# Raw input normalising in a convolution: ScalarE's copy and GpSimd's low part two rounds behind the subtract

## The chip, the core and the metric

The kernel runs on one core of a Trainium2 chip. TensorE (PE; PEld is its weight load) multiplies matrices into PSUM. VectorE (DVE), ScalarE (ACT) and GpSimd (POOL) do the elementwise work, and SyncE (SP) issues the DMA transfers. Each engine takes the instructions of its own queue in order, and an instruction that waits for another engine's signal holds up what is queued behind it. The metric is the device time of one execution in microseconds (us): the median over runs.

## The reference

The input x has 8 batches of 2048 positions with 512 channels. Two blocks follow each other, each with a residual:

```
x = x + layernorm(s4(layernorm(x)))      # a long convolution per channel, then gelu
x = x + layernorm(ffn(layernorm(x)))     # a gated recurrence over the 8 batches, then tanh
```

`s4` builds one filter of 2048 taps for each of the 512 channels from a state of 64 complex numbers, convolves every channel with its filter and applies gelu. The first layernorm runs over the 512 channels, so each position and batch has a mean and a factor 1/sqrt(var + eps); the convolution's input is (x - mean) * factor. The feed-forward part isn't touched by the change.

## The kernel before

Positions are cut into NJ = 16 chunks of 128. Channels are cut into NG = 16 groups of G = 32, and a group is two slices of HS = 16 channels. A convolution of one channel is the product with a 128 x 128 matrix of taps inside a chunk (tile `t`), plus what earlier chunks left in the state (tile `x`, 256 columns: 32 channels by 8 batches), which is spread over the chunk by a second matrix (tile `m`). The state goes from chunk to chunk: this is "the chain". Values are kept as two float16 halves, a high half, which ScalarE copies (L101), and a low half, which VectorE subtracts (L102); a product of two such values takes three matmuls (`mm3`, L450 to L452).

The main loop (L801) runs over the groups g. While group g is convolved, the kernel prepares the next ones: the chain and the taps of group g + 1, and the input of group g + 2. A group has 16 steps s_ (L838). In order, a step emits

- every second step, the gelu of the four channels before (`conv_out`, L717, ACT)
- one or more pieces of the input's normalising (`norm_x`, L844, the part that the change touches)
- the convolution of two channels (`conv_mm`), with the chain's products in between: `chain_hi` (L661) after the first, `chain_lo` after the second. `chain_lo` of step j is one more product (L667), which needs the low half of the state of step j - 1, and then the split of its result: ACT's copy (L101) and VectorE's subtract (L102)
- in steps 1 to 12 a doubling of the next group's taps (`tap_step`: three products, L101, L102)
- the first products of the next chain step (`chain_in`)
- pieces of work on the feed-forward weights, on ACT and VectorE: L404 and L405 in step 2, L408 and L409 in step 5, L392/L393 in steps 8 and 12, L446 in step 14

The input of a group comes in two transfers of 1 MB (`load_x`, L629), each into one of two `xg` buffers with 8 chunks. A buffer is free for the next group when the last low part that reads it is done. Normalising goes in 8 rounds of two chunks, four of them in each buffer. A round r has four parts: GpSimd subtracts the mean (part 0, L641), VectorE multiplies with the factor (part 1, L643), ScalarE copies the high half into `u` (part 2, L645), GpSimd subtracts to get the low half (part 3, L647; for group 2 VectorE does it). They depend on each other in this order.

The list `norms` (L837) holds the parts in the order in which they are emitted, and L844 takes from its head as the steps go on, two in each step. With the lags of the kernel before, sub r comes in step 2r, mul r in 2r + 1, copy r in 2r + 2 and low r in 2r + 3; in the last step, 15, come mul 7, low 6, copy 7 and low 7. In group 1 the list starts at step 3 (`ND1`, L843), as its first input comes late. Groups 14 and 15 have no input to prepare. GpSimd's queue has one more kind of work, two copies of taps for each group (`load_taps`, L683), which overwrite tiles that the products of the group before have read.

The queues of PE, ACT, VectorE and GpSimd follow the written order within a group; between the end of one group and the start of the next, and on SP, a scheduler sets it. So on GpSimd the second L683 and sub 0 and sub 1 of the next group stand ahead of low 7 of the old one.

Of the kernel before, what the change touches and what calls it, by code (L numbers as in the profile page):

```python
# [24 lines left out]
NJ = L // P  # L25
# [34 lines left out]
def s4_gated_block(ctx, tc, a, dbg=None):  # L60
# [445 lines left out]
    def early_tiles():  # L506

        ya = early["y"] = [cb.tile([P, 2, H // HS, 2, HS], F32, name="ya", tag="m", bufs=4) for _ in range(2)]
        xa = cb.tile([P, 2, 2, H], F32, name="xra", tag="t0", bufs=3)
        xb = FJ.tile([P, 2, H], F32, name="xr", tag="wl"), FE.tile([P, 2, H], F32, name="xrb", tag="y")  # L510
        for cj in range(QC):
            early[cj] = ya[cj % 2][:, cj // 2], xb[cj // 2] if cj % 2 else xa[:, cj // 2]
        for cj in (0, 2, 1, 3):
            dma(out=early[cj][1], in_=a["r"][0:2, cj * P : (cj + 1) * P].rearrange("t p h -> p t h"))
            dma(out=early[cj][0][:, 0:SE], in_=y_d[cj, :, 0:SE, 0:2])

    def early_y(sl, y):

        v = y.rearrange("p (c b) h -> p c b h", b=NB)
        for i in range(2):  # L520
            Q.tensor_copy(early["y"][i][:, :, sl], v[:, i:QC:2, 0:2])
# [56 lines left out]
    JP = 2  # L578
    MAN = {mybir.EngineType.PE, mybir.EngineType.Activation, mybir.EngineType.DVE, mybir.EngineType.Pool}
    with ExitStack() as cctx:  # L580
# [44 lines left out]
        def load_x(g):  # L625
            us[g] = (cb, cr, ce)[g % 3].tile([P, NJ, 2, G, NB], F16, name="u", tag=f"u{g % 3}", bufs=1)
            for jq in range(NJ // JQ):
                xg = cr.tile([P, JQ, G, NB], F32, name="xg")
                dma(out=xg, in_=a["xr"][jq * JQ : (jq + 1) * JQ, :, g].rearrange("j p h b -> p j h b"))  # L629
                xgs[g, jq] = xg  # L630
# [18 lines left out]
        def chain_in(g, j):  # L649

            if j == 0:
                xs_[g] = (ce, cb)[g % 2].tile([P, NJ - 1, 2, GB], F16, name="x", bufs=1)
            u = us[g].rearrange("p j i h b -> p j i (h b)")
            pxs[g, j] = px.tile([P, GB], F32, name="pxt")
            mm3(pxs[g, j], lambda i: bm16[:, i, :], lambda i: u[:, j, i, :], stop=(j == 0))
# [18 lines left out]
        def load_taps(g):  # L674

            for sl in (2 * g, 2 * g + 1):
                t0 = cb.tile([P, 2, P, HS], F16, name="t0", bufs=3)
                base = kpad[:, sl, 1 : P + 1, :]
                tap = bass.AP(base.tensor, base.offset, [[HS, P], [2 * P * H, 2], [1, P * HS]])
                dma(out=t0.rearrange("p i t h -> p i (t h)"), in_=tap)  # L680
                t0s[sl] = t0
                m = cb.tile([P, 2, HS, P], F16, name="m", bufs=4)
                Q.tensor_copy(m[:, :, :, 0:4].rearrange("p i h k -> p i k h"), mb[:, :, :, sl * HS : (sl + 1) * HS])  # L683
                ms[sl] = m
# [10 lines left out]
        def tap_steps(g):  # L695
            steps = [(lv, k) for lv in range(2, LEV) for k in range(0, 1 << lv, min(1 << lv, 512 // HS))]
            return [(sl, lv, k) for lv, k in steps for sl in (2 * g, 2 * g + 1)]
# [23 lines left out]
        def weights(w):  # L721

            i = WORDER.index(w)
            wts[w] = (FW if i < 2 else FV if i == 2 else FT).tile([P, 2, 7, 2, BP], F16, name=f"w{w}", bufs=1)
            d = dma(out=wts[w], in_=wf_d[i])

        def conv_last(g):

            u, x = us[g], xs_[g]
            yt = {}  # L730
            for j0, j1, hn in ((0, JF, HS), (JF, NJ, 4)):
                n = j1 - j0
                for sl in (2 * g, 2 * g + 1):
                    t0, m = t0s[sl], ms[sl]
                    if j0 == 0:
                        yt[sl] = cb.tile([P, NJ * NB, HS], F32, name="y")
                    y = yt[sl][:, j0 * NB : j1 * NB]
                    for h0 in range(0, HS, hn):
                        pyt = py.tile([P, hn, n * NB], F32, name="pyt")
                        for hm in range(h0, h0 + hn):  # L740
                            hg = sl % 2 * HS + hm
                            o, c = pyt[:, hm - h0], NB if j0 == 0 else 0
                            mm3(o, lambda i: t0[:, i, :, hm], lambda i: u[:, j0:j1, i, hg, :], stop=False)
                            mm3(o[:, c:], lambda i: m[:, i, hm, :],
                                lambda i: x[:, max(j0 - 1, 0) : j1 - 1, i, hg * NB : (hg + 1) * NB], start=False)
                        S.activation(y[:, :, h0 : h0 + hn], pyt.rearrange("p h c -> p c h"), AF.Gelu, scale=unsc)  # L746
                    if j0 == 0:
                        early_y(sl, yt[sl])
                    dma(out=y_d[j0:j1, :, sl].rearrange("j p b h -> p j (b h)"), in_=y.rearrange("p (j b) h -> p j (b h)", b=NB))
                if j0 == 0:  # L750
                    early_row(0, (1,))

            for i in range(2):
                pt = [pm_.tile([P, KT, P], F32, name="pmt") for _ in range(2)]
                forms(0, 0, i, [normed[i], normed[i + 2]], pt)()
            early_row(1)
            for cj in range(QC):
                dma(out=x1_d[cj, :, 0], in_=early[cj][1][:, 0])
# [42 lines left out]
        for g in range(NG):  # L801
            nxt, nn = g + 1 < NG, g < NG - 2
            ahead = g > 0 and nxt
            if g == 1:
                FJ = ctx.enter_context(tc.tile_pool(name="fj", bufs=1, side="right", reuse_waits="tile"))
                c0r = FJ.tile([P, H], F32, name="c0r")
                dma(out=c0r, in_=a["c0r"])
                puc = FJ.tile([P, 3, KT], F32, name="puc")
            if g == NG - 2:
                rctx.close()  # L810
                FW = ctx.enter_context(tc.tile_pool(name="fw", bufs=1, side="right", reuse_waits="tile"))
                for w in range(2):
                    weights(w)
            if not nxt:
                ectx.close()
                FV = ctx.enter_context(tc.tile_pool(name="fv", bufs=1, side="right", reuse_waits="tile"))
                FE = ctx.enter_context(tc.tile_pool(name="fe", bufs=1, side="right", reuse_waits="tile"))
                fcol = FE.tile([P, 4, KT], F32, name="fcol")
            with tc.manual_schedule(engines=MAN if nxt else MAN | {mybir.EngineType.SP}):
                if ahead:  # L820
                    load_taps(g + 1)
                    if g == NG - 2:
                        mctx.close()
                    taps = tap_steps(g + 1)
                    chain_in(g + 1, 0)
                if nn:
                    load_x(g + 2)
                if not nxt:
                    early_tiles()
                    for sl in (2 * g - 2, 2 * g - 1):  # L830
                        early_y(sl, ys[sl])
                    dma(out=fcol, in_=a["fcol"])
                    weights(2)
                    early_row(0, (0,))
                    conv_last(g)
                    continue
                norms = [(k - lag, part) for k in range(NJ // JP + 1) for part, lag in ((0, 0), (2, 1), (1, 0), (3, 1))]  # L837
                for s_ in range(NJ):  # L838
                    if s_ % 2 == 0 and s_:
                        conv_out(g, s_ // 2 - 1)  # L840
                    if nn:

                        d = ND1 if g == 1 else 0  # L843
                        while norms and s_ >= d and (s_ == NJ - 1 or len(norms) > 4 + 2 * NJ * (NJ - 1 - s_) // (NJ - d)):  # L844
                            norm_x(g + 2, *norms.pop(0))

                    conv_mm(g, 2 * s_)
                    if ahead and s_ < NJ - 1:
                        chain_hi(g + 1, s_)
                    conv_mm(g, 2 * s_ + 1)  # L850
                    if ahead and s_ < NJ - 1:
                        chain_lo(g + 1, s_)
                    if ahead and 1 <= s_ <= 12:
                        tap_step(*taps[s_ - 1])
                    if ahead and s_ < NJ - 2:
                        chain_in(g + 1, s_ + 1)
                    for f in work.get((g, s_), ()):
                        f()
                conv_out(g, NJ // 2 - 1)
# [495 lines left out]
```

## Time and profile before

| | us |
|---|---|
| median of 3 runs | 2872.67 |
| lowest and highest run | 2871.69, 2873.89 |
| span of the profiled execution | 2869.6 |
| busy in the span: PE / PEld / DVE / ACT / POOL | 2567.3 / 2236.0 / 2097.3 / 1478.7 / 1213.1 |
| stretch 0 to 143 (statistics of the input, first chains) | PE busy 72.7 |
| stretch 143 to 577 (convolution with normalising) | PE 364.2, DVE 348.1, ACT 286.6, POOL 309.7 |
| stretch 577 to 640 (last groups of the convolution) | PE 49.2 |
| stretch 640 to the end (feed-forward) | PE 2081.2, DVE 1612.2 |

In the stretch of the change the four parts take, as means of one instruction: L641 1455 ns (96 of them from 200 to 580 us), L643 926 ns, L645 630 ns, L647 1235 ns. The shortest L643 of the whole run took 676 ns, the longest 1783.

A line of a timeline reads: start and duration in us, engine, line, operation, tiles out and in, partitions x elements and types, how many instructions are merged in it, and in brackets how long the engine stood idle before it and what ended that. A line of the waits reads: engine, tile and line that waited, the instruction it waited for, us in total, how often, and the longest.

### The profile page before, as it was taken

To read this page: it belongs to the slowest core of one execution; us is meant where nothing else is said; L and a number is where in the kernel's file an instruction comes from. 1 tells how busy PE (TensorE), PEld (TensorE's weight loads), DVE (VectorE), ACT (ScalarE), POOL (GpSimd) and SP (SyncE) were. 2 spreads that over 40 slices of the span, in tenths; PEclk is the share of its full clock that TensorE was granted. 3 is DMA by queue.
4 is the path that set the end of the run, shared out by engine and by line. 5 is a ranking of instruction groups with operands and counts; after the bars stand their busy time and mean duration, and the time that the engine had idled before them with its cause. 6 is when DMAs were issued, how large, how long until landed. Compare 5 with 4: busy or idle time off the path is not lost.

```text
span 2869.6 us, 60008 instructions
## 1 busy us (share of the span) xinstructions
PE 2567.3 (89%) x23940; PEld 2236.0 (78%) x23940; DVE 2097.3 (73%) x4248; ACT 1478.7 (52%) x3091; POOL 1213.1 (42%) x1496
## 2 busy tenths in 40 slices
PE   4588888876999999999999998999999999999991
PEld 3377777765888888778888886888888788888880
DVE  7878788837667766677777777777777677776758
ACT  8966666634344444445455544455454445544435
POOL 5776777613112221114554531355444124443317
PEclk8799999987999999999999999999999999999995
DMA  6978887797324333224565532355564235543356
GB/s 232 312 233 261 254 263 247 243 263 204 112 65 115 103 93 92 78 89 138 152 174 151 141 100 89 106 161 165 147 163 140 85 89 152 151 130 100 89 163 244
DMA packets 521937, 451.10 MB, mean 157 GB/s; under 512 B 289974, under 2 KB 401080, under 8 KB 516664
## 3 DMA queue, kind: packets, MB, share of 16 engines
q1 hardware_dynamic: 521224, 446.74, 52.4%
q8 instruction: 187, 3.06, 0.4%
q14 instruction: 94, 0.77, 0.1%
q10 hardware_dynamic: 432, 0.52, 0.1%
HBM read 295.41 MB, written 151.78 MB: 156 GB/s over the span
## 4 chain that ended last, share of the span: by engine, by line
PE 34%; DVE 9%; ACT 3%; DMA 2%; issue 1%; POOL 1%; SPq 0%; POOLq 0%; ACTq 0%; DVEq 0%
PE u L950 32%; PE pt L485 1%; DVE u L992 1%; DVE gate L1036 1%; DVE cf L1051 1%; DMA z_d<-zc 1%; ACT xf L101 1%; DVE cd L1037 1%; ACT gate L1016 1%; DVE sth L462 1%; DVE zz L1174 1%; DVE sty L462 1%; ACT y L903 0%; DVE u2p L989 0%; DVE xf L102 0%
## 5 line engine op out<-in xcount | busy, mean ns | idle before, releaser
L950 PEld LDWEIGHTS <-w 128*128 128x128 f16 x15120 | 1482.5, 98 | 217.2 <-issue 28.3
L950 PE MATMUL u<-xf,w 128*128 128x256 f16 x8064 | 947.6, 274 | 30.7 <-ACT zt L1003 12.7
L950 PE MATMUL u<-cf,w 128*128 128x256 f16 x7056 | 826.2, 273 | 3.8 <-DVE cf L1051 3.8
L988 ACT ACTIVATE u2p<-u 128x256 f32<-128x256 f32 x256 | 96.4, 378 | 449.8 <-PE u L950 449.6
L950 PE MATMUL u<-w,xf 128*128 128x256 f16 x2688 | 314.4, 275 | 14.8 <-DVE u L992 4.8
L989 DVE TENSOR_TENSOR u2p<-u2p,u 128x256 f32<-128x256 f32 x256 | 106.8, 417 | 285.8 <-ACT u2p L988 284.3
L1141 POOL TENSOR_TENSOR x1r<-x1r,zr 128x512 f32<-128x512 f32 x96 | 132.7, 1382 | 426.8 <-ACT zr L1140 309.4
L1016 ACT ACTIVATE gate<-u,bias 128x512 f32<-128x512 f32 (+1 forms) x384 | 200.5, 574 | 217.0 <-PE u L950 217.0
L950 PEld LDWEIGHTS <-xf 128*128 128x128 f16 x2688 | 264.6, 99 | 49.5 <-issue 10.7
L904 POOL TENSOR_TENSOR xr<-y,xr 128x512 f32<-128x512 f32 x120 | 160.4, 1357 | 308.2 <-ACT y L903 308.2
L992 DVE TENSOR_TENSOR u<-u,u2p 128x512 f32<-128x512 f32 x256 | 179.0, 699 | 8.8
L647 POOL TENSOR_TENSOR u<-xg,u 128x512 f16<-128x512 f32 x104 | 128.8, 1242 | 114.0 <-ACT u L645 113.9
L471 POOL TENSOR_TENSOR rsy<-rsy,nhalf 128x2 f32<-128x2 f32 (+1 forms) x68 | 50.9, 748 | 296.7 <-DVE rsy L465 284.4
L641 POOL TENSOR_TENSOR xg<-xg,mu 128x512 f32<-128x512 f32 x112 | 162.7, 1459 | 6.0 <-DMA xg<-in_xr 6.0
L102 DVE TENSOR_TENSOR x<-pxt,x 128x256 f16<-128x256 f32 x240 | 100.0, 418 | 63.2 <-ACT x L101 62.3
L1123 POOL TENSOR_TENSOR zr<-zr,ur 128x512 f32<-128x512 f32 x96 | 129.7, 1351 | 22.4 <-DMA zr<-z_d 16.6
L1021 DVE SCALAR_TENSOR_TENSOR gate<-gate,gate 128x1024 f32<-128x1024 f32 x64 | 93.4, 1459 | 59.8 <-ACT gate L1016 59.0
L462 DVE BATCH_NORM_STATS2 sty<-y 128x6 f32<-128x512 f32 x120 | 76.7, 681 | 72.7 <-DMA y<-y_d 72.7
L101 ACT ACTIVATE x<-pxt 128x256 f16<-128x256 f32 x240 | 91.5, 382 | 74.1 <-PE pxt L667 68.4
L101 ACT ACTIVATE xf<-pt 128x512 f16<-128x512 f32 x124 | 60.7, 489 | 133.4 <-DVE xf L102 114.4
L667 PE MATMUL pxt<-x,at 128*128 128x256 f16 x224 | 61.8, 276 | 75.1 <-DVE x L102 73.9
L450 PE MATMUL pyt<-u,t 128*128 128x128 f16 (+2 forms) x544 | 121.4, 223 | 5.4 <-ACT y L746 5.4
(371 smaller groups left out, 5319.1 us busy)
## 6 DMA issues: line engine op xcount, KB each, us to landing
xs<-in_rr SPq DMA_DIRECT2D x32, 1024.0 KB, 5.7
t<-kpad SPq DMA_DIRECT2D x32, 1024.0 KB, 5.6
y_d<-y SPq DMA_DIRECT2D x30, 1024.0 KB, 7.6
xr<-in_r SPq DMA_DIRECT2D x60, 512.0 KB, 5.5
xa<-x_d SPq DMA_DIRECT2D x120, 256.0 KB, 4.1
y<-y_d SPq DMA_DIRECT2D x59, 512.0 KB, 5.7
x_d<-xr SPq DMA_DIRECT2D x59, 512.0 KB, 3.2
xg<-in_xr SPq DMA_DIRECT2D x28, 1024.0 KB, 8.7
```

What stands on the lines that cost most here:

```text
L101: S.activation(hi, src, AF.Copy)
L450: T.matmul(out, lhsT=w(0), rhs=x(0), start=start, stop=False)
L462: V.bn_stats(st[:, i], v)
L641: Q.tensor_tensor(xg, xg, bc(mu1), ALU.subtract)
L647: (V if g == 2 else Q).tensor_tensor(u[:, js, 1], xg, u[:, js, 0], ALU.subtract)
L904: Q.tensor_tensor(xv, yv, xv, ALU.add)
L950: T.matmul(u[:, d], lhsT=w(f, b, i == 1, k), rhs=x(f, b, i == 2, k), start=opens and bank not in seen, stop=stop and j == len(n) - 1, skip ...
L989: V.tensor_tensor(u2, u2, u[:, UY], ALU.add)
L992: V.tensor_tensor(u[:, 2:4], u[:, 2:4], u2[:, None].to_broadcast([P, 2, BP]), ALU.add)
L1016: act = lambda o, s_, b: S.activation(o, s_, AF.Tanh, scale=gsc[kind], bias=b)
L1123: Q.tensor_tensor(s_["z"], s_["z"], us_[c], ALU.add)
L1141: Q.tensor_tensor(s_["x"], s_["x"], s_["z"], ALU.add)
```

## The change

The list of parts gets one more round, its order within a round changes, parts that don't exist are left out of the list, and the threshold of L844 loses its 4, as the list has 32 entries now for 36 before:

```
-norms = [(k - lag, part) for k in range(NJ // JP + 1) for part, lag in ((0, 0), (2, 1), (1, 0), (3, 1))]
+norms = [(k - lag, part) for k in range(NJ // JP + 2) for part, lag in ((2, 2), (0, 0), (1, 0), (3, 2)) if 0 <= k - lag < NJ // JP]
...
-    while norms and s_ >= d and (s_ == NJ - 1 or len(norms) > 4 + 2 * NJ * (NJ - 1 - s_) // (NJ - d)):
+    while norms and s_ >= d and (s_ == NJ - 1 or len(norms) > 2 * NJ * (NJ - 1 - s_) // (NJ - d)):
```

Worked out for a group from 2 to 13, step by step (s sub, m mul, c copy, l low):

```
step    0     1     2     3     4     5     6     7     8     9     10    11    12    13    14    15
before  s0    m0    s1c0  m1l0  s2c1  m2l1  s3c2  m3l2  s4c3  m4l3  s5c4  m5l4  s6c5  m6l5  s7c6  m7l6 c7l7
after   s0m0  s1m1  c0s2  m2l0  c1s3  m3l1  c2s4  m4l2  c3s5  m5l3  c4s6  m6l4  c5s7  m7l5  c6l6  c7l7
```

In the queues that result, PE's is the same. On GpSimd sub 0, sub 1 and sub 2 of the next group stand ahead of low 7 of the old one, and sub 4 stands ahead of low 2. On ACT copy 7 and the last gelu of a group stand ahead of the next group's first chain copy, which was ahead of them before. On SP the store of `y` (L719) and the load of L445 change places.

## The prediction

> **What bounds the kernel now.** I read the page for the span, then busy time by stretch, then who waited for whom within the convolution, and last the timelines of TensorE, VectorE, GpSimd and the load queue through one channel group. X(k) stands for the start of the chain's last product (L667) of step k, "mul r", "sub r", "copy r" and "low r" for L643, L641, L645 and L647 of round r, xlo(k) for the L102 subtract that X(k+1) needs.
>
> ```profile
> span 2869.6 us, 60008 instructions
> ```
>
> ```profile
> 293.50:325.05 31.55, 26.65 (x319) 22.96 (x318) 25.48 (x45) 21.01 (x46) 22.67 (x20) 1.00 0.82 255
> ```
>
> The second line is one channel group: length, then busy us (and instructions) of PE, PEld, DVE, ACT, POOL, then granted clock, DMA share, GB/s. Five such stretches in a row measure 31.50 to 31.55 us; the groups repeat like a clock, at a granted clock of 1.00, so one group can be worked out and multiplied. PE stands idle for 4.9 us of it. From 143 to 577 us, where the changed code runs, the waits are:
>
> ```profile
> ACT u L645 <- DVE xg L643: 69.5, 64, 1.8
> PE pxt L667 <- DVE x L102: 64.4, 61, 4.0
> ...
> DVE xg L643 <- POOL xg L641: 13.0, 13, 3.0
> ```
>
> ACT's copy waits 69.5 us for the multiply, PE waits 64.4 us for xlo, and the two look like one thing. The timelines say that they are not:
>
> ```profile
> 295.20 0.27 PE L667 MATMUL pxt<-x,at 128*128 128x256 f16 x1 [0.16 <-DVE x L102]
> ...
> 298.12 0.27 PE L667 MATMUL pxt<-x,at 128*128 128x256 f16 x1 [1.02 <-DVE x L102]
> ...
> 302.57 0.27 PE L667 MATMUL pxt<-x,at 128*128 128x256 f16 x1 [1.36 <-DVE x L102]
> ```
>
> ```profile
> 293.12 1.00 DVE L446 SCALAR_TENSOR_TENSOR un<-un,c0r 128x512 f32<-128x512 f32 x1
> 294.05 0.08 DVE L446 DVE_READ_ACCUMULATOR un<-un,c0r 128x1 f32 x1
> 294.05 0.77 DVE L643 TENSOR_TENSOR xg<-xg,rs 128x512 f32<-128x512 f32 x1
> 294.74 0.41 DVE L102 TENSOR_TENSOR x<-pxt,x 128x256 f16<-128x256 f32 x1
> 295.98 1.75 DVE L643 TENSOR_TENSOR xg<-xg,rs 128x512 f32<-128x512 f32 x1 [0.84 <-POOL xg L641]
> 297.65 0.41 DVE L102 TENSOR_TENSOR x<-pxt,x 128x256 f16<-128x256 f32 x1
> ```
>
> ```profile
> 292.41 1.16 POOL L647 TENSOR_TENSOR u<-xg,u 128x512 f16<-128x512 f32 x1 [2.42 <-ACT u L645]
> 293.51 1.24 POOL L683 COPY m<-mb 128x128 f16<-128x128 f16 x1
> 294.34 2.85 POOL L641 TENSOR_TENSOR xg<-xg,mu 128x512 f32<-128x512 f32 x2
> 297.14 2.74 POOL L647 TENSOR_TENSOR u<-xg,u 128x512 f16<-128x512 f32 x2
> 299.84 1.46 POOL L641 TENSOR_TENSOR xg<-xg,mu 128x512 f32<-128x512 f32 x1
> ```
>
> What ends last ahead of X(1), X(2) and X(4) is VectorE's queue: a multiply stands right before xlo. In this boundary between two groups the multiply at 294.05 is mul 7 of the old group and the one at 295.98 is mul 0 of the new one, which waits 0.84 us for sub 0 and then takes 1.75 us where others take 0.68, until sub 1 is over at 297.19. Other pairs read alike: L405 starts at 300.08 inside a GpSimd subtract (299.84 to 301.30) and takes 1.50 us, its sister L409 0.42. L102, which reads PSUM, stays at 0.41. So an operation of VectorE on two SBUF operands is held up while GpSimd works; that is the price list for the change.
>
> **The change part by part.** Eight multiplies, subtracts, copies and lows per group stay, and PE's queue is the same. Copy r and low r keep their steps (2r+2 and 2r+3, the last at 15). Sub and mul go one round ahead: mul r sat at step 2r+1 and now sits at 2r-1, with mul 0 at step 0 and mul 1 at step 1. On VectorE the places of the multiplies stay the same; each place has the next round's. Groups 2 to 13, twelve of them, are alike. All times below are on the clock of the timelines above.
>
> 1. *ACT's wait goes.* It is worth nothing. The copy that waited 1.23 us ran 302.22 to 302.85; the next in ACT's queue, the chain's own copy, started at 302.88, which is 0.31 after X(4)=302.57, the same lag as after 298.12 (298.42). It waited for PE, and PE for VectorE. Price if the cover were gone: up to the 64.4 us that PE waits.
>
> 2. *Sub 7 leaves step 13.* L393 (289.37 to 291.05, then mul, then xlo) overlapped it from 289.37 to 289.98. With GpSimd free there X(14), which waited 1.23 us, comes 0.6 earlier: 291.45 for 292.05. Between 0 and 0.6; I take 0.6.
>
> 3. *Mul 0 now stands before xlo(0), where mul 7 stood without a wait.* It waits for sub 0, which stands behind L683, which overwrites taps that the old group's last products read; those end with ACT's release at 293.02, now about 292.45. L683's spacing to the subtract is 0.83 (293.51 to 294.34): sub 0 from 293.3. One subtract takes 1.27 to 1.64 (294.34 to 295.98): mul 0 from 294.6 to 294.9. Sub 1 and sub 2 follow at once on GpSimd, so the nearest row is the 1.75 above: done by 296.5. From the start of xlo to X is 0.46 (294.74 to 295.20), so X(1) is 296.8 to 297.0 for 295.20, +1.7. Least: 0.68 for mul 0, +0.6. Queued behind mul 0 is xlo(0), and PE for it.
>
> 4. *Mul 1 stands before xlo(1)*, with sub 2 running: 0.68 to 1.75, so X(2) is 298.3 to 298.9 for 298.12 (before, the 0.84 wait and mul 0's 1.75 lay here). I take +0.6.
>
> 5. *Step 3: L404, L405, mul 2, xlo(3).* Before, GpSimd fell idle at 301.30 until low 1 at 302.92, which waited for the copy, which waited for mul 1; so mul 1 ran free in 0.68. Now copy 1 has its input long since and GpSimd has low 0, sub 3 and low 1 in a row, so each of the three VectorE operations may meet one. Nothing in the trace shows that place so filled. By the free rows +0, by the 1.75 row against 0.68 for the multiply +1.1 and by shifted overlaps of L404 and L405 +0.6 more. I take +1.3, nearer the filled row, since GpSimd is never idle there now. X(4): 304.5, +1.9.
>
> 6. *The second half's load.* Sub 4 needs the second xg buffer, freed by low 7. L629 issued it at 298.77, just when low 7 ended, and issues of that line in the groups beside it landed 7.3, 7.6, 8.7 and 8.9 us later; sub 4 started at 307.52, 8.75 after, so even now there is hardly room.
>
> ```profile
> 298.77 1.92 SPq L629 DMA_DIRECT2D xg<-in_xr  x1
> ```
>
> Now sub 4 is due a round sooner, right after low 1, while low 7 stands behind sub 2 and ends some 0.7 later (299.5). It lands at 306.8 to 308.4, sub 4 ends 1.27 later, mul 4 needs 0.68 to 1.75 before xlo(7), and X(8) is at least 309.2 to 311.9, for 309.37: -0.2 to +2.5. This delays the same xlo as part 5, so it is not added: the greater counts, and I take 2.0 for both. Behind the waiting sub 4 stand low 2, sub 5 and L683; on SP nothing new waits, only y's store and L445 change places.
>
> 7. *Step 9*, L393 and mul once more behind a shifted GpSimd: 0 to +0.6; I take 0. The first changed group (group 1, whose load is late anyway, a 3.99 us wait of PE) has mul 1 a step sooner: 0 to +1.3, I take 0.5. Group 0 has no chain: 0.
>
> Sum: 12 x 2.0 + 0.5 = 24.5 us on a span of 2869.6, so 2894.1. The median of the runs, 2872.67, lies 3.1 over the span; the same 3.1 gives 2897. After 577 us nothing changes, and nothing there makes up for a late start: it is one long run of PE (93% busy from 640 us on).
>
> [...]
>
> **The rivals.** *A, faster: the new waits are hidden.* Mul 0 gets its turn before sub 1 (+0.6 at X(1)), xlo(1) is then earlier than before, and only part 2 is left: 12 x -0.6 = -7, so 2866. For it: the 1.02 and 1.36 us of PE's waits at X(2) and X(4) are there to be eaten. Against: in the row shown sub 1 waits for nothing and was ahead, and mul 0 took 1.75 us. It decides if mul 0's mean at the boundary falls under 1 us and sub 4 does not wait. *B, no change:* the gain of part 2 pays for a stall of about 0.6 a group; 2868 to 2878. Against it: X(1) alone has 1.7. *C, the load rules:* each round of the load ends in a stall at X(8) at the long landing (2.5) and step 9 adds 0.6: 12 x 3.1 + 1.3 = 38.5, so 2911. For it: 8.75 us of the 8.9 are used up now. That the change doesn't do what it says I leave out: the built order of the engines has the multiplies one round ahead.
>
> **How the numbers follow.** Forecast 0.68, A 0.13, B 0.07, C 0.12. The likeliest gives 2897. Bounds of the forecast: 12 x 0.8 = 10 over (parts 3 to 5 at their least with a landing of 8.1) to 12 x 2.9 + 1 = 36 over: 2883 to 2909. Widened towards B and C: 2874 to 2912, which leaves out A, half of B and the end of C. This kernel's runs tell about 0.2% (5.7 us) from no change: faster 0.13, same 0.07, slower 0.80.
>
> **What would show it.** ACT's wait for L643 falls from 69.5 us to under 10, with no gain on PE; DVE's wait for L641 grows from 13 us to 25 or more; POOL's wait for the load grows from 6.0 us to over 20; the wait before X(1) grows from 0.16 to about 1.8 and that before X(14) falls from 1.23 to 0.6; the group's period is 33.5. I am wrong if the period stays under 31.6: then mul 0 found its subtract done, or the chain had slack that I don't see.

## The result, and the profile after

The changed kernel takes 2885.54 us (median of 5 runs, 2880.99 to 2886.13) against 2872.67 (5 runs, 2868.53 to 2874.30): 1.0043 times, with an interval of 1.003 to 1.0055. It is slower, by 12.9 us, where the prediction said 24. The profiled execution spans 2883.8 us, 14.2 more than the one before.

The waits of the changed kernel from 140 to 600 us (who waited for whom, us in total, times, longest):

```profile
ACT x L101 <- PE pxt L667: 143.9, 121, 3.5
...
PE pxt L667 <- DVE x L102: 69.5, 57, 4.1
...
POOL xg L641 <- DMA xg<-in_xr: 38.8, 13, 7.3
DVE xg L643 <- POOL xg L641: 21.4, 20, 3.0
...
ACT u L645 <- DVE xg L643: 4.6, 3, 3.9
```

ACT's wait for the multiply is gone (69.5 before, 4.6 now), and nothing was won by it: ACT now waits in the chain's own copy (143.9), and PE's wait for xlo is larger than before (64.7 in the same window). GpSimd waits for the second half's load in each group. TensorE through the changed kernel's X(8) of one group and X(14), X(1) and X(4) of the next:

```profile
284.83 0.27 PE L667 MATMUL pxt<-x,at 128*128 128x256 f16 x1 [1.26 <-DVE x L102]
...
298.84 0.27 PE L667 MATMUL pxt<-x,at 128*128 128x256 f16 x1 [0.75 <-DVE x L102]
...
304.02 0.27 PE L667 MATMUL pxt<-x,at 128*128 128x256 f16 x1 [2.18 <-DVE x L102]
...
310.16 0.27 PE L667 MATMUL pxt<-x,at 128*128 128x256 f16 x1 [1.36 <-DVE x L102]
```

X(14) of the kernel before:

```profile
292.05 0.27 PE L667 MATMUL pxt<-x,at 128*128 128x256 f16 x1 [1.23 <-DVE x L102]
```

Against the rows of before, the wait at X(14) fell from 1.23 to 0.75, the one at X(1) rose from 0.16 to 2.18, the one at X(2) (1.02) is gone, the one at X(4) (1.36) is as it was here, and X(7) or X(8) has a new one in eight of the twelve groups. VectorE, the same two groups:

```profile
282.81 1.63 DVE L643 TENSOR_TENSOR xg<-xg,rs 128x512 f32<-128x512 f32 x1 [1.53 <-POOL xg L641]
...
301.90 1.74 DVE L643 TENSOR_TENSOR xg<-xg,rs 128x512 f32<-128x512 f32 x1 [1.18 <-POOL xg L641]
...
303.89 1.43 DVE L643 TENSOR_TENSOR xg<-xg,rs 128x512 f32<-128x512 f32 x1
...
307.67 1.50 DVE L405 TENSOR_TENSOR ws<-wl 128x256 f32<-128x256 f32 x1
309.09 0.68 DVE L643 TENSOR_TENSOR xg<-xg,rs 128x512 f32<-128x512 f32 x1
```

and GpSimd:

```profile
281.50 1.28 POOL L641 TENSOR_TENSOR xg<-xg,mu 128x512 f32<-128x512 f32 x1 [4.27 <-DMA xg<-in_xr]
...
300.26 4.51 POOL L641 TENSOR_TENSOR xg<-xg,mu 128x512 f32<-128x512 f32 x3
304.73 2.73 POOL L647 TENSOR_TENSOR u<-xg,u 128x512 f16<-128x512 f32 x2
307.42 1.46 POOL L641 TENSOR_TENSOR xg<-xg,mu 128x512 f32<-128x512 f32 x1
309.16 1.62 POOL L647 TENSOR_TENSOR u<-xg,u 128x512 f16<-128x512 f32 x1 [0.28 <-ACT u L645]
```

The row at 301.90 is mul 0: it waits 1.18 us for sub 0 and is then held for 1.74 us beside subs 1 and 2, and xlo(0) and PE wait behind it. The row at 303.89 is mul 1, held beside sub 2 and low 7. The row at 309.09, mul 2, runs free in 0.68 us: sub 3 ended at 308.88, and GpSimd waited for copy 1 until 309.16. The row at 281.50 is sub 4, 4.27 us late because of the load; mul 4 (282.81) waits for it, and X(8) (284.83) for mul 4.

So that kernels can be compared by place, the table cuts a group at the starts of L667. Each number is a mean over the twelve groups 2 to 13, read from the timeline of TensorE. "Half clock" counts the groups in which PE ran at half its clock (granted 0.50) for 3.4 us, of which more below. The medians stand against 2868.4 to 2868.8 us for the kernel before in the same runs on the chip; only the first two rows are from the runs of the result.

| kernel | median us | ratio, 95% interval | X(14) to X(1) | to X(2) | to X(4) | to X(10) | to X(14) | group | half clock |
|---|---|---|---|---|---|---|---|---|---|
| before | 2872.67 | 1 | 3.18 | 2.92 | 4.45 | 11.81 | 9.19 | 31.55 | 0 |
| after | 2885.54 | 1.0043, 1.003 to 1.0055 | 5.17 | 1.91 | 4.26 | 12.50 | 8.72 | 32.55 | 5 |
| sub 7 only | 2862.05 | 0.9977, 0.9968 to 0.9986 | 3.12 | 2.87 | 4.45 | 11.85 | 8.72 | 31.02 | 0 |
| mul 0 first | 2887.92 | 1.0061, 1.0049 to 1.0074 | 5.97 | 1.96 | 4.00 | 11.81 | 9.19 | 32.93 | 8 |
| short load | 2875.14 | 1.0016, 1.0007 to 1.0025 | 5.17 | 1.98 | 4.19 | 11.95 | 8.72 | 32.00 | 8 |
| subs ahead | 2891.2 | 1.0078, 1.0065 to 1.009 | 3.13 | 2.87 | 5.51 | 13.12 | 8.72 | 33.34 | 9 |
| muls 0, 1 later | 2887.92 | 1.0068, 1.0056 to 1.0081 | 2.83 | 2.36 | 5.96 | 13.17 | 8.72 | 33.04 | 8 |
| late slots | 2855.9 | 0.9956, 0.9943 to 0.9969 | 3.64 | 1.72 | 4.46 | 12.24 | 8.39 | 30.45 | 0 |
| subs first | 2873.25 | 1.0017, 1.0008 to 1.0026 | 3.64 | 1.72 | 5.55 | 12.36 | 8.39 | 31.66 | 6 |
| L393 free | 2849.83 | 0.9932, 0.9919 to 0.9946 | 3.64 | 1.73 | 4.46 | 10.87 | 9.26 | 29.96 | 0 |
| L405 free | 2847.56 | 0.992, 0.9907 to 0.9934 | 3.64 | 1.73 | 3.37 | 11.68 | 9.27 | 29.68 | 0 |

After against before: +1.99 at X(1), -1.01 at X(2), -0.19 at X(4), +0.69 up to X(10), -0.47 at X(14), in all 1.00 us a group and 12 us in twelve. Besides, group 1 ended 2.7 us later (X(14) at 199.85 for 197.12), with sub 0 of its first load 3.6 us later (173.90 for 170.29); of the 14.7 us in all, 0.5 were made up behind group 13, which leaves the 14.2. Little of the 2.7 seems to be the change's: the nine other kernels below have the changed order in group 1, and reached that X(14) between 195.89 and 198.34, 197.4 on the mean.

### The profile page after: what moved, and what is told of

It is laid out like the page before. It is cut to its first block, busy times and chain, and to the rows that moved or that the text cites. A ratio compares the mean times of both kernels' runs of the same rounds, so it can differ in the third digit from the quotient of the medians.

```text
span 2883.8 us, 60021 instructions
## 1 busy us (share of the span) xinstructions
PE 2575.4 (89%) x23940; PEld 2241.5 (78%) x23940; DVE 2099.1 (73%) x4248; ACT 1471.4 (51%) x3091; POOL 1214.5 (42%) x1496
## 4 chain that ended last, share of the span: by engine, by line
PE 33%; DVE 9%; ACT 3%; DMA 2%; issue 2%; POOL 1%; SPq 0%; POOLq 0%; ACTq 0%; DVEq 0%
PE u L950 31%; PE pt L485 1%; DVE u L992 1%; DVE gate L1036 1%; DVE zz L1174 1%; ACT xf L101 1%; DVE cd L1037 1%; DVE sth L462 1%; DVE cf L1051 1%; ACT gate L1016 1%; DMA z_d<-zc 0%; ACT y L903 0%; DVE u2p L989 0%; DVE sty L462 0%; DVE xf L102 0%
## 5 line engine op out<-in xcount | busy, mean ns | idle before, releaser
L950 PE MATMUL u<-xf,w 128*128 128x256 f16 x8064 | 948.0, 274 | 31.5 <-ACT zt L1003 12.9
L641 POOL TENSOR_TENSOR xg<-xg,mu 128x512 f32<-128x512 f32 x112 | 165.4, 1488 | 38.8 <-DMA xg<-in_xr 38.8
L647 POOL TENSOR_TENSOR u<-xg,u 128x512 f16<-128x512 f32 x104 | 135.3, 1306 | 86.2 <-ACT u L645 86.2
L1123 POOL TENSOR_TENSOR zr<-zr,ur 128x512 f32<-128x512 f32 x96 | 129.8, 1352 | 20.1 <-DMA zr<-z_d 14.2
L667 PE MATMUL pxt<-x,at 128*128 128x256 f16 x224 | 62.8, 280 | 80.9 <-DVE x L102 79.0
L643 DVE TENSOR_TENSOR xg<-xg,rs 128x512 f32<-128x512 f32 x112 | 113.2, 1011 | 21.4 <-POOL xg L641 21.4
```

Source lines behind the costliest of these rows:

```text
L641: Q.tensor_tensor(xg, xg, bc(mu1), ALU.subtract)
L643: V.tensor_tensor(xg, xg, bc(rs1), ALU.mult)
L647: (V if g == 2 else Q).tensor_tensor(u[:, js, 1], xg, u[:, js, 0], ALU.subtract)
L950: T.matmul(u[:, d], lhsT=w(f, b, i == 1, k), rhs=x(f, b, i == 2, k), start=opens and bank not in seen, stop=stop and j == len(n) - 1, skip ...
L1123: Q.tensor_tensor(s_["z"], s_["z"], us_[c], ALU.add)
```

## The experiments

All but the short load are the changed kernel with the order of the parts in groups 2 to 13 written out as a table; group 1 keeps the changed order. The lines taken out are those of the kernel before where nothing else is said.

```diff
-                    if nn:
+                    if nn and g > 1:
+                        for jp_, part_ in SCHED[s_]:
+                            norm_x(g + 2, jp_, part_)
+                    elif nn:
...
```

In the tables s, m, c, l are sub, mul, copy and low of a round, in steps 0 to 15.

**Sub 7 only** (part 2 of the prediction by itself).

```diff
 step  12          14
-      s6 c5       s7 c6
+      s6 c5 s7    c6
```

> The kernel before with one move in groups 2 to 13: sub 7 at step 12 (behind sub 6) for step 14. Theory: L393 at step 12 no longer overlaps a GpSimd subtract, 1.2 us for 1.70, PE's wait before X(14) falls from 1.22 to 0.75 and the time by 12 x 0.48 = 6, about 2867. Rival (X(14) waits for ACT's side, or the 0.5 us is lost at the next wait): 2872 to 2873.

It is 0.23% faster, 6.6 us by the ratio, with a group of 31.02 us for 31.55, as the theory had it. L393 ran in 1.23 us for 1.70 (the first row is of the kernel before), and the wait at X(14) is that of the changed kernel, 0.75 us:

```profile
289.37 1.70 DVE L393 SCALAR_TENSOR_TENSOR wq<-ws,wq 128x1024 f16<-128x1024 f32 x1 [0.26 <-ACT wq L392]
319.70 1.23 DVE L393 SCALAR_TENSOR_TENSOR wq<-ws,wq 128x1024 f16<-128x1024 f32 x1 [0.26 <-ACT wq L392]
```

All else is as before, ACT's wait for L643 included (63.7 us). So the change has this gain in it, and the 12.9 us are what is left after it.

**Mul 0 first** (part 3 by itself).

```diff
 step  0        1
-      s0       m0
+      s0 m0
```

> The kernel before with one move in groups 2 to 13: mul 0 at step 0, ahead of xlo(0), for step 1. Theory: X(1) comes 2.9 us later, since mul 0 still ends at sub 1's end, X(2) 1.5 later, as xlo(1) has no multiply ahead of it now; 12 x 1.5 = 18, about 2890. Rival (the late load is what costs in the changed kernel, and this move has no part in it, as sub 4 keeps its step): 2873.

0.61% slower, 17.5 us by the ratio, as the theory had it: X(1) comes 2.79 us later and X(2) 1.83. PE's wait at X(1) is 3.05 us. VectorE at the boundary:

```profile
297.25 0.76 DVE L644 TENSOR_TENSOR xg<-xg,rs 128x512 f32<-128x512 f32 x1
299.17 1.74 DVE L644 TENSOR_TENSOR xg<-xg,rs 128x512 f32<-128x512 f32 x1 [1.16 <-POOL xg L642]
```

Here mul 7 and mul 0 both stand ahead of xlo(0). The wait of 1.16 us for sub 0 and the 1.74 us of mul 0 are the changed kernel's 1.18 and 1.74. By the trace (a group of 32.93 us for 32.55) this one move costs more than the whole change, which takes mul 7 out of that place and has sub 7's gain; the intervals of the two ratios overlap.

**The short load** (part 6).

```diff
 def load_x(g):
...
-    dma(out=xg, in_=a["xr"][jq * JQ : (jq + 1) * JQ, :, g].rearrange("j p h b -> p j h b"))
+    j0 = JQ - 1 if jq and g > 3 else 0
+    dma(out=xg[:, j0:], in_=a["xr"][jq * JQ + j0 : (jq + 1) * JQ, :, g].rearrange("j p h b -> p j h b"))
...
-    Q.tensor_tensor(xg, xg, bc(mu1), ALU.subtract)
+    src = xgs[g, 1][:, JQ - 1 :].to_broadcast([P, JP, G, NB]) if g > 3 and jp >= NJ // JP // 2 else xg
+    Q.tensor_tensor(xg, src, bc(mu1), ALU.subtract)
```

> The changed kernel, but for groups from 4 on the second transfer of a group brings one chunk of the eight, and the subtracts of rounds 4 to 7 read that chunk alone, with the same shapes; the rest of the second half's input is left out. Theory: the late load costs 0.7 us a group; without it GpSimd's wait for the load falls from 38.8 us to under 10 and the time is 10 x 0.73 = 7 lower than the changed kernel, about 2878. Rival (the boundary alone costs the 13 us, the load's wait is hidden): 2885.

0.16% slower than before instead of 0.43%. GpSimd's wait for the load fell from 38.8 us (13 times) to 7.9 (4 times). X(4) to X(10) went from 12.50 to 11.95, most of the way to the 11.81 of before; the rest of the group is the changed kernel's. The load costs 0.55 us a group, 12 x 0.55 = 6.6 us, about half of the change's loss, and the theory held. The two means mix groups at full and at half clock, though (eight at half clock here, five in the changed kernel): between X(4) and X(10), groups at full clock differ by 0.49 us and those at half clock by 0.40, so 0.4 to 0.5 is the safer price.

**Subs ahead** (the changed kernel's subtracts with the multiplies, copies and lows of before).

```diff
 step  0     1     2     3     4     5     6     7     8     9     10    11    12    13    14    15
-      s0    m0    s1c0  m1l0  s2c1  m2l1  s3c2  m3l2  s4c3  m4l3  s5c4  m5l4  s6c5  m6l5  s7c6  m7l6c7l7
+      s0    s1m0  c0s2  m1l0  c1s3  m2l1  c2s4  m3l2  c3s5  m4l3  c4s6  m5l4  c5s7  m6l5  c6l6  m7c7l7
```

> Groups 2 to 13 with the subtracts at the changed kernel's steps and the multiplies, copies and lows at the steps of the kernel before. Theory (the place of the multiply on VectorE's queue decides, ACT's wait costs nothing): ACT's wait for L643 is back at 60 us or more, X(14) keeps the 0.5 us that sub 7 gives by leaving step 13, X(1) is as before, and the load is late for GpSimd only, as mul 4 has its old step: 12 x -0.4 = -5, about 2868. Rival (ACT's wait holds the chain up): with the wait back nothing is gained on the kernel before, 2873 or more.

(Low 6 stands one step earlier than before, at 14.) A miss: 0.78% slower, 22 us. ACT's wait for L643 is back (75.6 us), and the time lies where the rival had it, but not for the rival's reason: X(14) to X(2) is as with sub 7 alone, and the loss lies at X(4) and behind it. VectorE and GpSimd ahead of X(4):

```profile
306.89 1.74 DVE L644 TENSOR_TENSOR xg<-xg,rs 128x512 f32<-128x512 f32 x1
```

```profile
306.65 1.44 POOL L642 TENSOR_TENSOR xg<-xg,mu 128x512 f32<-128x512 f32 x1
```

Sub 3 starts 0.24 us ahead of mul 1, which stands for 1.74 us where it took 0.68 before: +1.06 at X(4), whose wait is 2.42. That is the filled place that part 5 of the prediction spoke of, with the price that it gave (1.1). What comes behind X(4) wasn't in any theory; busy time and granted clock (last but two) in stretches of 2 us show it:

```profile
309.00:311.00 2.00, 1.98 (x20) 1.84 (x20) 1.42 (x4) 0.84 (x3) 1.16 (x1) 0.68 0.77 265
311.00:313.00 2.00, 2.00 (x14) 1.59 (x13) 0.79 (x3) 1.09 (x3) 1.28 (x1) 0.50 0.00 0
```

After the wait of 2.42 us PE runs at half its clock from 309.7 to 313.1. Nine of the twelve groups have such a stretch and last 33.70 us, three have none and last 32.28: 1.42 us each, 9 x 1.42 = 13 of the 22 us. Those three also lost 0.46 us between X(4) and X(10) (12.27 for 11.81); which wait that was, no run here takes apart.

**Muls 0 and 1 later** (the changed kernel, parts 3 and 4 undone; the lines taken out are the changed kernel's).

```diff
 step  0        1        2
-      s0 m0    s1 m1    c0 s2
+      s0       s1 m0    c0 s2 m1
```

> The changed kernel with mul 0 back at step 1 and mul 1 at step 2; everything else of it stays. Theory (the 2.0 us at X(1) is mul 0 waiting for sub 0 ahead of the chain's subtract, and part of it came back at X(2)): from X(14) to X(1) 3.15 us instead of 5.17, from X(1) to X(2) 2.9 instead of 1.9, X(14) to X(4) 10.5 instead of 11.3, so some 0.8 us a group, 12 x 0.8 = 10 us: ratio to the kernel before about 1.001 instead of 1.0043. Rival (three subtracts in a row on GpSimd stretch mul 1 wherever it stands, so that the loss only moves on to X(3) and X(4)): 1.004, no gain.

The rival held in what it said of the time: the loss moved. It is not mul 1 that is stretched more, though (1.30 us for 1.43), but mul 2. X(14) to X(2) is 5.19 us for the changed kernel's 7.08, and X(2) to X(4) is 5.96 for 4.26. VectorE and GpSimd ahead of X(4):

```profile
306.70 1.75 DVE L644 TENSOR_TENSOR xg<-xg,rs 128x512 f32<-128x512 f32 x1
```

```profile
306.46 1.44 POOL L642 TENSOR_TENSOR xg<-xg,mu 128x512 f32<-128x512 f32 x1
```

Mul 2 ran free in the changed kernel and takes 1.75 us here, beside sub 3. Taking the stall of X(1) away makes VectorE early enough to meet sub 3 again. PE then waits 2.60 us ahead of X(4), and eight groups fall to the half clock (33.51 us on the mean against 32.09 in the four others). Without it this order would be some 0.5 us a group better than the changed one (32.09 for 32.55): the theory had the stall's place right and its return wrong.

**Late slots** (a try at a version that beats both: multiplies out of the places that PE waits for).

```diff
 step  8     9     10    11        12        13    14    15
-      s4c3  m4l3  s5c4  m5l4      s6c5      m6l5  s7c6  m7l6c7l7
+      s4c3  l3s5  m4    m5c4s6    m6l4c5s7  l5c6  m7l6  c7l7
```

> Rounds 0 to 3 as in the kernel before, rounds 4 to 7 ahead of it: the multiplies of the late rounds leave the places that PE waits for (beside L393 in steps 9 and 13, and step 15) for steps 10, 11, 12 and 14, and sub 7 stands at step 12. Theory (only the operations that stand between a product of PE and the chain's subtract in a step where VectorE is late cost time, each its own length): X(10) 0.68 us earlier, X(14) 0.47 + 0.68, X(1) at most 0.16: 1.85 to 2.0 us a group, 12 x 1.9 = 23 us faster than before, ratio 0.992. Rival (GpSimd is too full from step 10 on, its subtracts now lie beside the multiplies and L393 and stretch them to 1.5 us and more): the gain of sub 7 alone or less, 0.998 to 1.00.

0.44% faster than before, 12.5 us, half of what was expected. PE no longer waits at X(14), but X(14) to X(1) is 0.46 us longer, with L446 at 1.87 us for 1.00, and the wait at X(10) rose from 0.88 to 1.35. VectorE and GpSimd there:

```profile
305.48 2.90 DVE L393 SCALAR_TENSOR_TENSOR wr<-wl,wr 128x512 f16<-128x512 f32 x2
```

```profile
305.15 2.95 POOL L642 TENSOR_TENSOR xg<-xg,mu 128x512 f32<-128x512 f32 x2
```

Subs 5 and 6 run as soon as GpSimd's queue reaches them, a place in the table notwithstanding, and hold the two L393, which took 1.83 us in the same place before.

**Subs first** (the late slots, and the first half's subtracts in a row; the lines taken out are the late slots').

```diff
 step  0     1   2     3     4     5     6     7     8     9
-      s0    m0  s1c0  m1l0  s2c1  m2l1  s3c2  m3l2  s4c3  l3s5
+      s0s1  m0  s2s3  m1    c0    m2l0c1  m3l1c2  l2c3  s4l3  s5
```

> The last one, and besides all four subtracts of the first half in a row at the start of the group, copies 0 to 2 and lows 0 to 2 later, so that GpSimd stands idle while L405 and mul 1 run in step 3. Theory (L405 takes 1.50 us only for the GpSimd subtract beside it): L405 0.42 us, X(4)'s wait 1.36 falls to 0.3, one more us a group than the run beside it: ratio 0.988. Rival (the four subtracts reach to L404 and L405 anyway, or the lows that were put off collide with the multiplies of steps 5 and 6): the same as the run beside it, 0.992, or slower.

The rival again: the subtracts reach to 297.52, a low follows at once, L405 still takes 1.38 us and mul 1 now 1.66; the wait at X(4) is 2.45 us, and six groups fall to the half clock.

**L393 free** (the late slots, with GpSimd kept from running ahead by a low that waits; the lines taken out are the late slots').

```diff
 step  8       9     10    11        12
-      s4c3    l3s5  m4    m5c4s6    m6l4c5s7
+      s4c3s5  l3    m4    m5c4l4s6  m6c5s7
```

> The late slots again, with subs 4 and 5 both right after low 2 and sub 6 only behind low 4, so that GpSimd stands idle in step 9, where L393 took 2.90 us beside two subtracts instead of 1.83. Theory (the half of the expected gain that the late slots did not bring lay in that stretched L393): L393 back to 1.7 to 1.8 us, the wait before X(10) from 1.35 to 0.3 at most, the group's period from 30.51 to 29.4 us: 12 x 2.1 = 25 us faster than the kernel before, ratio 0.991. Rival (another wait takes its place, for the second half's load or for sub 6 ahead of mul 6): 0.995, as with the late slots alone.

0.68% faster than before, 19.5 us. The two L393 take 1.36 us, and X(10) has no wait; a smaller one came in its place, 0.77 us at X(13), where mul 6 waits for sub 6 (0.23 us) and then takes 1.76 beside sub 7.

**L405 free** (the same, and subs 2 and 3 behind low 1; the lines taken out are those of the run before).

```diff
 step  4     5     6     7     8
-      s2c1  m2l1  s3c2  m3l2  s4c3s5
+      c1    l1s2  m2s3  c2    m3l2s4s5
```

with c3 and l3 in step 9.

> The last one, and besides subs 2 and 3 put behind low 1, which itself waits for copy 1, and multiplies 2 and 3 at steps 6 and 8, so that GpSimd stands idle when L405 runs in step 3. Theory: L405 0.42 us instead of 1.50, the wait before X(4) from 1.36 to 0.3 at most, one us a group more than the run beside it: ratio 0.987. Rival (the rounds of the first half are now bunched, multiplies 2 and 3 wait for their subtracts ahead of the chain in steps 6 and 8): the same as the run beside it or slower, 0.991 to 0.996.

0.8% faster than before, 23 us by the ratio, the best of the study; its interval overlaps that of the run before it. VectorE and TensorE:

```profile
292.80 0.41 DVE L405 TENSOR_TENSOR ws<-wl 128x256 f32<-128x256 f32 x1
...
297.11 1.37 DVE L408 TENSOR_TENSOR ws<-ws,wl 128x256 f32<-128x256 f32 x1
```

```profile
299.92 0.27 PE L668 MATMUL pxt<-x,at 128*128 128x256 f16 x1 [0.73 <-DVE x L102]
```

L405 in 0.41 us takes 1.09 off X(2) to X(4), as expected. Most of it goes again in this new wait at X(7): the subtracts that were moved away from L405 now lie beside L408, which takes 1.37 us for 0.61.

## Why the prediction was right or wrong

The direction and the mechanism held, a stall ahead of X(1) and a late load; the size was twice too large, 2.0 us a group for a measured 1.00, and the time came out near the lower end (2883) of what the forecast allowed itself. The 2.9 us a group of its upper end no run shows: this kernel lost 1.00, and the order that lost most, subs ahead, 1.79. On the prediction's clock, against its own numbers:

| | forecast | measured |
|---|---|---|
| X(14) | -0.6 | -0.47 |
| X(1) | +1.7 | +1.52 |
| X(2) | +0.6 | +0.51 |
| X(4) | +1.9 | +0.32 |
| X(8) | +2.0 | +0.84 |
| X(10) | +2.0 | +1.01 |

- **Part 1**, ACT's wait is worth nothing: right as far as the runs show. It fell by 65 us and PE's wait rose; sub 7 only is faster with nearly all of the wait left (63.7 us). No run takes the wait away and nothing else.
- **Part 2**, sub 7: right in kind, 0.47 for 0.6, and shown alone, as 6.6 us.
- **Part 3**, mul 0 ahead of xlo(0): right, and shown alone by the kernel that moves only mul 0.
- **Part 4**, mul 1: right; the old waits ahead of X(2) came back as slack.
- **Part 5**, +1.3 ahead of X(4): wrong for this kernel; X(2) to X(4) takes 4.46 us in the groups at full clock, and 4.45 before. The size is right for a place in which GpSimd is busy: subs ahead, subs first and muls 0 and 1 later have it, +1.06, +1.1 and +1.5. The step that failed is "GpSimd is never idle there now". Because of the stall of part 3 VectorE comes to mul 2 10.25 us behind X(14), and by then sub 3 is over (10.04) and low 1 has to wait 0.28 us for copy 1; with muls 0 and 1 later it comes at 9.02, with sub 3 running to 10.22. So the two prices exclude each other: with part 3 undone, that of part 5 appeared. When mul 2 began, no operation of GpSimd's was running, and it took 0.68 us; beside one, mul 2 took 1.75 us with muls 0 and 1 later.
- **Part 6**, the load: right in kind, too large. Sub 4 waited for it in all twelve groups and started 6.6 to 8.7 us after the load's issue (7.3 on the mean), where landings of 7.3 to 8.9 were forecast and 2.0 at X(8) taken, near the long end. The 8.9 among the prediction's rows is a load of the first half (issued at 311.30); those of the second half landed after 7.1 to 8.7 us in the kernel before. It cost 0.69 behind X(4), most of which went when the load was cut. That "on SP nothing new waits" was wrong, with little effect: the issue of L445 takes 3.5 to 6.0 us there, for 0.35 before, and in group 3 it holds the load's issue back to 8.30 us behind X(14), for 7.5 in the other groups. As part 5 came to nothing, part 6 alone would have been the better forecast: at 1.15, the middle of its -0.2 to +2.5 (an estimate from the prediction's landings and multiplies), 12 x 1.15 + 0.5 = 14.3 us, or 2887.
- **Part 7**, step 9 and group 1: step 9 is within 0.3 (the wait at X(10) was 0.87 to 1.16 us for 0.88). Group 1 was 2.7 us for 0.5 in the profiled execution, but 0.3 on the mean of the nine other kernels.

Two readings of the prediction are off without effect: low 6 doesn't keep step 15 but goes to 14, and 69.5 us (64 times) is ACT's wait in a slightly longer stretch than 143 to 577 us, in which it is 68.8 (63 times).

Of the signs named, DVE's wait for L641 reached 21.4 us, not 25, and the period 32.55 us, not 33.5; both follow from parts 5 and 6. That PE could fall to a lower clock was in no part of the prediction. It did so in five groups of the changed kernel and cost nothing that can be seen: X(14) to X(4) takes 11.28 to 11.45 us there against 11.31, because VectorE was the later one at X(4) anyway.

## What to carry to other kernels

A wait off the path that sets the end can be worth nothing (ACT's fell by 65 us here, and nothing was won), and a dependency relaxed by one round puts the operation that was waited for into a new place: price that place, by what stands behind it in its queue and by what the other engine does at that moment. When two stalls follow each other, the first can decide whether the second exists, as that of X(1) did here for X(4), so their prices mustn't be added unseen. The order that won did the plain thing: it took the free-moving operations out of the few steps in which VectorE is late, and used a low that waits for its copy to keep GpSimd from running ahead into those steps.

## What the runs showed of the hardware

- **PE fell to half its clock (granted 0.50) after some of the waits of 2.2 to 3.1 us, and which ones went by where the wait lay.** Granted clock of the changed kernel in stretches of 2 us:

```profile
334.00:336.00 2.00, 0.00 (x0) 0.00 (x0) 1.95 (x2) 0.00 (x0) 2.00 (x3) 1.00 0.94 203
336.00:338.00 2.00, 1.81 (x22) 1.56 (x22) 1.93 (x4) 1.52 (x4) 2.00 (x2) 0.88 1.04 363
338.00:340.00 2.00, 2.00 (x17) 1.68 (x16) 1.33 (x4) 0.57 (x3) 2.00 (x3) 0.50 1.16 346
340.00:342.00 2.00, 2.00 (x25) 1.90 (x24) 2.00 (x3) 1.06 (x4) 1.01 (x1) 0.77 1.00 270
```

  After the wait of 2.18 us that ends at 336.2, products of 256 columns take 0.42 us for 0.27, from 337.5 on for 3.4 us. No kernel whose longest wait in a group is 1.37 us or less has such a stretch in groups 2 to 13; with one of 2.2 to 3.1 us five to nine groups of twelve have it. Behind X(1) it was hidden in the changed kernel (11.28 to 11.45 us from X(14) to X(4) for 11.31), behind X(4) it cost 1.2 to 1.4 us.

  Which groups are hit can be read from the traces. All 44 stretches in groups 2 to 13 last 3.41 us, and within a kernel they start whole multiples of 3.41 us apart: in the changed kernel at 238.54, 337.53, 368.25, 433.10 and 532.09 us, that is 29, 9, 19 and 29 steps. Taken in such steps, each of the eleven traces shows the same: after a step in which PE was idle for at least 58.7% the next one ran at half clock (44 of 44), and after none with at most 57.7% did it. In the step from 334.11, which holds nearly the whole wait, PE was busy for 1.36 us of 3.41. The equally long wait ahead of X(1) at 304.02 falls across the border at 303.39, the two steps keep 1.80 and 2.68 busy us, and the clock stays. The ends of PE's products are modelled in a trace, so these shares are estimates.
- **Beside GpSimd's operations more of VectorE's took longer than the multiply**: L393 2.90 us for 1.36 (two of 128x512), L408 1.37 for 0.42, L446 1.87 for 0.80. Beside subs that followed each other without a wait, the multiply took 1.74 us, 1.06 more than the free 0.68, where one subtract took 1.25 to 1.44. Not every overlap did this: mul 2 at 309.09 took 0.68 us, with low 1 beside it from 309.16 on.
